# Own rows of layer 0 gathered as the unit three ahead opens, their transposes placed later in the order

## The chip, the cores and the metric

The program runs on one core of one Trainium2 chip, in one launch. The metric is the device time of that core in microseconds (us); below it is better. The kernel before was run three times without the profiler, and its time is the median of the three.

## The reference, cut to what matters

Two graph layers are computed for 8 batches of 2048 nodes with 256 channels, over one adjacency matrix with few neighbours per node (and each node its own neighbour). Each layer ends in a residual sum and a layer norm.

```python
# layer 0: scores are x W1 W2^T x^T on the edges, values are x W3
e = einsum('bnd,bmd->bnm', x @ W1, x @ W2)
e = where(adj > 0, leaky_relu(e, 0.2), -1e12)
x = layernorm(x + relu(softmax(e) @ (x @ W3)))
# layer 1: four heads of 64, scores a_src.q_i + a_dst.q_j on the edges
q = (x @ W).reshape(B, N, 4, 64)
e = where(adj > 0, leaky_relu(e_src_i + e_dst_j, 0.2), -9e15)
x = layernorm(x + elu(softmax(e) @ q))
```

## The kernel before

**Tiling.** The nodes are sorted by degree and cut into 16 tiles of 128 nodes, one node per partition. A tile `t` has `SLOTS[t]` neighbour slots, from 12 for the sparsest tile to 36 for the densest. The batches are taken in two halves `h` of four. A *unit* is one (layer, half, tile): units 0 to 15 are layer 0 of the first half, from 12 slots up to 36, units 16 to 31 layer 0 of the second half, again from 12 to 36, and then 32 units of layer 1. `K` is the unit's number of slots.

**A unit of layer 0.** `before0` gathers the tile's own 128 rows (4 KB each, tile `xo`) with an indirect DMA on POOL, copies them to the residual tile `xr` with four DMAs on SP (L531), transposes them on PE with eight 128x128 transposes (L417, tile `ps_t_x`), lets ACT copy these out (`xT`, L419), multiplies by `A` = W1 W2^T on PE (L427) and lets ACT copy the result `g` out (L542). `logits0` takes, for each slot, four dot products of the gathered neighbour rows with `g` on DVE (L562), and then a softmax. `sums0` adds up the neighbour rows with these weights on PE (L639), 16 small matmuls a slot, for which ACT makes four diagonal tiles `dg` a slot (L659). `after0` multiplies by W3, adds the residual, normalises, makes the table rows of layer 1 and writes them.

**The ring.** Neighbour rows (tile `s`) are gathered by POOL into a ring of 16 tiles of two slots (L196 is the shared gather helper). A ring tile is free again when PE has summed its slots, so POOL's gathers wait for PE (`POOL s L196 <- PE acc L639`), and DVE's dot products follow the gathers.

**The order of the work.** The program is written as generators that are stepped by `tick` (L955). A tick first lets `pump` issue ring gathers as far as there are credits, then emits up to two slots of dot products, then steps each of three lists once (twice, if the list holds more than one entry): `starts` (the `before0` of coming units), `ends` (the `after0` of finished ones) and `lists` (the neighbour lists). `sums0` emits one slot's sums and then a tick. `before0` of unit j + 3 is put into `starts` when half of unit j's slots are summed (L990), gathers at its first step, and steps four times (L534) before its transposes. POOL's order is the order in which the program emits (L346). [...] The pool of `xo` has two buffers (L170), that of `xr` three (L171). A new tile takes a buffer whose last use is over.

Of the kernel before, what the change touches and what calls it, by code (L numbers as in the profile page):

```python
# [11 lines left out]
F32 = mybir.dt.float32  # L12
# [10 lines left out]
P = 128  # L23
# [17 lines left out]
LATE = 6  # L41
# [88 lines left out]
def fast_path(  # L130
# [26 lines left out]
    NT = N // P  # L157
    KC = C // P
    HB = B // 2
    HC = HB * C  # L160
# [9 lines left out]
    xop = ctx.enter_context(tc.tile_pool(name="xown", bufs=2))  # L170
# [20 lines left out]
    def wide_tile(name):  # L191
        return wp.tile([P, 2 * QW], F32, tag="t", name=name)

    def gather(dst, table, index):

        nc.gpsimd.indirect_dma_start(  # L196
            out=dst, out_offset=None, in_=table, in_offset=AT(ap=index, axis=0),
            bounds_check=table.shape[0] - 1, oob_is_err=False,
        )
# [12 lines left out]
    xg = [tc.dram_tile([N, HC], F32, name=f"xg_{h}") for h in range(2)]  # L212
# [102 lines left out]
    order = const.tile([P, NT], I32, tag="order", name="order")  # L315
# [32 lines left out]
    def checks():  # L348

        worst = wide_tile("worst")[:, :P]  # L350
        nc.gpsimd.memset(worst, 0.0)
        bad = const.tile([P, NT + 3], F32, tag="bad", name="bad")
        found, known = bad[:, NT + 1 : NT + 2], bad[:, NT + 2 : NT + 3]
        nc.vector.tensor_scalar(bad[:, :NT], degs, 0.5, None, ALU.is_lt)
        listless = wide_tile("listless")[:, :total]
        nc.vector.tensor_scalar(listless, neg, 0.0, 0.0, ALU.is_lt, ALU.add, accum_out=found)
        nc.vector.tensor_reduce(known, degs, AX.X, ALU.add)
        nc.vector.tensor_tensor(known, known, found, ALU.add)
        nc.vector.tensor_scalar(bad[:, NT : NT + 1], known, float(total), None, ALU.not_equal)
        nc.vector.tensor_reduce(worst[:, 0:1], bad[:, : NT + 1], AX.X, ALU.max)  # L360
        yield
        pb = ps_tile("ps_bad")
        nc.tensor.transpose(pb[:, :P], worst, ident)
        yield
        most = const.tile([P, 1], F32, tag="most", name="most")
        nc.vector.tensor_reduce(most[0:1, :], pb[0:1, :P], AX.X, ALU.max)
        nc.vector.tensor_copy(flag, most[0:1, :])
        yield
        nc.vector.scalar_tensor_tensor(half, half, 2.0 * N, orderR, ALU.mult, ALU.add)
        for h in range(2):  # L370
            for j in range(2):
                nc.vector.tensor_scalar(
                    oidx[:, h, j], half, float((h * HB + j) * N), None, ALU.add
                )
# [37 lines left out]
    def transposed(src, name, dst):  # L412

        for i in range(2):
            pt = ps_tile(f"ps_t_{name}_{i}")
            for j in range(4):
                nc.tensor.transpose(pt[:, ts(j, P)], src[:, ts(4 * i + j, P)], ident)  # L417
            yield
            nc.scalar.copy(dst[:, ts(i, 512)], pt)  # L419
        yield  # L420

    def projected(srcT, weight, name, evict):
        for i in range(2):
            pp = ps_tile(f"ps_p_{name}_{i}")
            for j in range(2):
                for k in range(KC):
                    nc.tensor.matmul(  # L427
                        pp[:, ts(j, C)],
                        lhsT=srcT[:, ts((2 * i + j) * KC + k, P)],
                        rhs=weight[:, k, :],  # L430
                        start=(k == 0),
                        stop=(k == KC - 1),
                    )
            yield
            evict(i, pp)
        yield

    class Unit:
        def __init__(self, layer, h, t):
            self.layer, self.h, self.t = layer, h, t  # L440
            self.K = SLOTS[t]
            self.name = f"{layer}_{h}_{t}"

            n = self.K if self.K <= RING * CHUNK * 3 // 4 else -(-self.K // 2)
            self.parts = [(k, min(n, self.K - k)) for k in range(0, self.K, n)]
            self.chunks = [[] for _ in self.parts]
            self.p = [None] * len(self.parts)
            self.ps = [None] * len(self.parts)

            self.m, self.s = [], []  # L450
            self.ready = False


# [7 lines left out]
    clock = [0]  # L461
# [31 lines left out]
    def neighbours(t):  # L493
        K, o = SLOTS[t], offs[t]
        while t not in loaded:
            yield
        v = loaded[t].bitcast(I16)[:, :N]
        if t in up[:3]:
            numbered(loaded[t])
            nc.vector.memset(loaded[t][:, N // 2 :], 0.0)  # L500


        some = sp.tile([P, 8 * BLOCKS], F32, tag="some", name=f"some_{t}", bufs=2)
        for i in range(BLOCKS):
            nc.vector.max(some[:, ts(i, 8)], v[:, N * i // BLOCKS : N * (i + 1) // BLOCKS])
            if i % 8 == 7:
                yield
        credits[0] += 1
        rounds = -(-K // 8)
        m = sp.tile([P, 40], F32, tag="m", name=f"m_{t}")  # L510
        for i in range(rounds):
            nc.vector.max(m[:, ts(i, 8)], some)
            if i + 1 < rounds:
                nc.vector.match_replace(some, m[:, ts(i, 8)], some, 0.0)
            yield
        nc.vector.tensor_scalar(neg[:, o : o + K], m[:, :K], 0.5, LOWEST, ALU.is_lt, ALU.mult)
        far = sp.tile([P, 40], F32, tag="far", name=f"far_{t}", bufs=2)[:, :K]
        nc.vector.tensor_scalar(far, m[:, :K], 0.5, FAR, ALU.is_lt, ALU.mult)
        nc.vector.scalar_tensor_tensor(
            idx[:, o : o + K], m[:, :K], 1.0, far, ALU.subtract, ALU.add  # L520
        )
        listed[t] = True


    def before0(u):
        xo = xop.tile([P, HC], F32, tag="xo", name=f"xo_{u.name}")
        gather(xo, xg[u.h][:, :], order[:, u.t : u.t + 1])
        u.xr = xrp.tile([P, 2, HW], F32, tag="xr", name=f"xr_{u.name}")
        for r in range(2):
            for c in range(2):  # L530
                nc.sync.dma_start(  # L531
                    u.xr[64 * c : 64 * c + 64, r, :], xo[64 * r : 64 * r + 64, ts(c, HW)]
                )
        for _ in range(4):  # L534
            yield
        xT = wide_tile(f"xT_{u.name}")
        yield from transposed(xo, f"x_{u.name}", xT)
        while scored[0] < u.index - 1:
            yield
        u.g = gp.tile([P, HC], F32, tag="g", name=f"g_{u.name}")  # L540
        yield from projected(
            xT, w.A, f"g_{u.name}", lambda i, pp: nc.scalar.copy(u.g[:, ts(i, 512)], pp)  # L542
        )
        u.ready = True
# [369 lines left out]
    units = [Unit(0, h, t) for h in range(2) for t in up]  # L914
# [19 lines left out]
    for j, u in enumerate(units):  # L934
        u.index = j
    before = (before0, before1)
    logits = (logits0, logits1)
    sums = (sums0, sums1)
# [8 lines left out]
    def finish(u):  # L947
        yield from after[u.layer](u)
# [6 lines left out]
    def tick(limit):  # L955
        pump()
        while late and late[0][0] <= clock[0]:
            late.popleft()[1]()
        for _ in range(2):
            if ahead[0] < limit:  # L960
                ahead[0] += next(stream, 0)
        for queue in queues:
            for _ in range(min(len(queue), 2)):
                if queue and next(queue[0], queue) is queue:
                    queue.popleft()
        clock[0] += 1
# [5 lines left out]
    for j, u in enumerate(units):  # L972
        begun = False
        if 0 < j and j + 2 < NT:
            lists.append(neighbours(up[j + 2]))
        if j == NT:
            ends.append(checks())
        while len(ends) > 1:
            tick(0)
        if 2 <= j < 10:  # L980
            b, i = divmod(j - 2, 2)
            n = ts(i, N // 2)

            nc.gpsimd.dma_start(xg[1][n, ts(b, C)], x[HB + b, n])
        left = float(u.K)
        for share in sums[u.layer](u):
            ahead[0] -= share
            left -= share
            tick(left + units[min(j + 1, len(units) - 1)].K + LEAD)
            if not begun and left <= u.K / 2 and j + 3 < len(units):  # L990
                begun = True
                v = units[j + 3]
                starts.append(before[v.layer](v))
        ends.append(finish(u))
# [300 lines left out]
```

## Time and profile before

| what | value |
|---|---|
| time, median of three runs | 2709.94 us (2703.99 to 2711.37) |
| time of the profiled execution | 2598.36 us |
| its span, first to last instruction | 2596.3 us |
| DVE busy | 2148.3 us (83%) |
| PE busy | 1816.4 us (70%) |
| POOL busy | 1532.3 us (59%) |
| ACT busy | 1441.4 us (56%) |
| gathers of own rows, `xo` | 32, on POOL |
| gathers of neighbour rows in layer 0 | 596, on POOL |

In the span, about the first 95 us are setup, layer 0 of the first half runs to about 800 us, layer 0 of the second half to about 1595 us, and layer 1 to the end.

How to read the lines: a wait line is `engine tile line <- releaser: us in total, times, longest`. A window line gives, for a stretch of the span, the busy time of each engine and its instructions, the share of full speed that TensorE's clock was granted (PEclk), and the mean busy share of the 16 DMA engines. A timeline line gives start, duration, engine, source line, operation, output<-inputs, a count of merged instructions, and in brackets the idle time of the engine ahead of it and who ended it. `PEld` is the weight load of a matmul.

### The profile page before, as it was taken

To read this page: it belongs to the slowest core of one execution; us is meant where nothing else is said; L and a number is where in the kernel's file an instruction comes from. 1 tells how busy PE (TensorE), PEld (TensorE's weight loads), DVE (VectorE), ACT (ScalarE), POOL (GpSimd) and SP (SyncE) were. 2 spreads that over 40 slices of the span, in tenths; PEclk is the share of its full clock that TensorE was granted. 3 is DMA by queue.
4 is the path that set the end of the run, shared out by engine and by line. 5 is a ranking of instruction groups with operands and counts; after the bars stand their busy time and mean duration, and the time that the engine had idled before them with its cause. 6 is when DMAs were issued, how large, how long until landed. Compare 5 with 4: busy or idle time off the path is not lost. (4 is left out here: it accounts for less than half of the span.)

```text
span 2596.3 us, 52231 instructions
## 1 busy us (share of the span) xinstructions
PE 1816.4 (70%) x16675; PEld 989.4 (38%) x16675; DVE 2148.3 (83%) x7073; ACT 1441.4 (56%) x4849; POOL 1532.3 (59%) x1486
## 2 busy tenths in 40 slices
PE   1167797878778787788888878756475666764774
PEld 0145464545445455455555544212121222221221
DVE  6799899899889677777788885789888788988896
ACT  6245475656566556655666657454356556643455
POOL 3464455555555444535455555677677777776774
PEclk9588898989888788988898989878788788887877
DMA  9898787888875566767788768898799999987993
GB/s 382 276 338 273 257 313 267 302 285 280 269 270 194 186 218 240 247 231 235 255 264 284 257 206 273 301 342 327 273 341 355 349 339 367 349 320 270 325 358 106
DMA packets 249419, 734.92 MB, mean 283 GB/s; under 512 B 63200, under 2 KB 72544, under 8 KB 246704
## 3 DMA queue, kind: packets, MB, share of 16 engines
q0 software_dynamic: 192512, 645.89, 70.4%
q1 hardware_dynamic: 55360, 84.44, 9.6%
q8 instruction: 135, 2.21, 0.3%
q14 instruction: 148, 1.21, 0.1%
q10 hardware_dynamic: 1264, 1.18, 0.1%
HBM read 708.35 MB, written 76.09 MB: 302 GB/s over the span
## 5 line engine op out<-in xcount | busy, mean ns | idle before, releaser
L562 DVE CUSTOM_DVE_ANT_0 j<-s,g 128x256 bf16<-128x256 f32 x2384 | 1007.7, 423 | 197.7 <-DMA s<-xg,idx 127.2
L196 POOL DMA_INDIRECT s<-xg,idx x596 | 634.3, 1064 | 625.4 <-PE acc L639 413.5
L639 PE MATMUL acc<-s,ident 64*64 64x512 f32 x4768 | 610.9, 664 | 350.9 <-issue 296.7
L639 PE MATMUL acc<-s,dg 64*64 64x256 f32 x9536 | 706.1, 418 | 187.7 <-ACT dg L659 176.1
L196 POOL DMA_INDIRECT s<-qg,idx x596 | 606.7, 1018 | 242.0 <-issue 130.4
L659 ACT ACTIVATE dg<-twice,e 128x64 f32<-128x64 f32 x2384 | 617.6, 337 | 107.3 <-PE acc L639 101.8
L840 DVE TENSOR_TENSOR s<-s,p 128x2048 f32<-128x2048 f32 (+1 forms) x260 | 574.0, 2229 | 0.0
L639 PEld LDWEIGHTS acc<-s,dg 64*64 64x64 f32 x9536 | 383.1, 144 | 452.1 <-ACT dg L659 256.3
L639 PEld LDWEIGHTS acc<-s,ident 64*64 64x64 f32 x4768 | 210.4, 149 | 743.8 <-issue 600.0
L836 ACT ACTIVATE s<-s,e 128x64 f32<-128x64 f32 x1408 | 342.7, 335 | 47.7 <-DVE e L804 39.6
L395 ACT ACTIVATE z<-st,roots 128x4 f32<-128x4 f32 x64 | 19.1, 298 | 410.1 <-DVE st L384 410.1
L562 DVE DVE_READ_ACCUMULATOR2_ANT e<- 128x1 f32 x2384 | 194.0, 81 | 0.0
L204 POOL DMA_INDIRECT out_dram<-o,oidx x128 | 130.6, 1020 | 68.1 <-ACT o L407 32.2
L774 DVE TENSOR_TENSOR e<-s,own 128x32 f32<-128x32 f32 (+1 forms) x306 | 55.7, 186 | 121.5 <-DMA s<-qg,idx 120.3
L417 PE MATMUL ps_t_x<-ident,xo 128*128 128x128 f32 x256 | 55.4, 359 | 120.0 <-DMA xo<-xg,order 120.0
L723 PE MATMUL ps_q<-wqs,x1T 128*128 128x264 f32 x512 | 137.8, 407 | 2.1 <-ACT x1T L419 2.1
L427 PE MATMUL ps_p_h<-w_sb,hT 128*128 128x256 f32 x512 | 130.4, 399 | 5.6 <-ACT hT L419 5.6
L427 PE MATMUL ps_p_g<-A,xT 128*128 128x256 f32 x512 | 131.9, 404 | 1.8 <-ACT xT L419 1.5
L427 PEld LDWEIGHTS ps_p_g<-A,xT 128*128 128x128 f32 x512 | 98.0, 199 | 32.0 <-issue 8.1
L427 PEld LDWEIGHTS ps_p_h<-w_sb,hT 128*128 128x128 f32 x512 | 94.4, 194 | 40.8 <-issue 13.2
L723 PEld LDWEIGHTS ps_q<-wqs,x1T 128*128 128x128 f32 x512 | 98.3, 199 | 29.6 <-issue 7.7
L407 ACT ACTIVATE o<-xr,nmr,rstd 128x256 f32<-128x256 f32 x128 | 66.5, 589 | 76.1 <-DVE nmr L403 67.7
(138 smaller groups left out, 1467.9 us busy)
## 6 DMA issues: line engine op xcount, KB each, us to landing
adj<-in_adj_dram SPq DMA_DIRECT2D x16, 1024.0 KB
xr<-xo SPq DMA_DIRECT2D x128, 128.0 KB
x1s<-y SPq DMA_DIRECT2D x32, 512.0 KB
xr<-x1s SPq DMA_DIRECT2D x32, 512.0 KB
s<-xg,idx POOLq DMA_INDIRECT x596
s<-qg,idx POOLq DMA_INDIRECT x596
edges<-adj SPq DMA_DIRECT2D x16, 512.0 KB
xg<-in_x_dram SPq DMA_DIRECT2D x4, 2048.0 KB
```

The lines of the kernel that those rows point to most:

```text
L196: nc.gpsimd.indirect_dma_start(out=dst, out_offset=None, in_=table, in_offset=AT(ap=index, axis=0), bounds_check=table.shape[0] - 1, oob_i ...
L204: ins = nc.gpsimd.indirect_dma_start(out=table, out_offset=AT(ap=index, axis=0), in_=src, in_offset=None)
L407: nc.scalar.activation(dst[:, b, :], y[:, b, :], AF.Identity, bias=nmr[:, b : b + 1], scale=rstd[:, b : b + 1],)
L417: nc.tensor.transpose(pt[:, ts(j, P)], src[:, ts(4 * i + j, P)], ident)
L427: nc.tensor.matmul(pp[:, ts(j, C)], lhsT=srcT[:, ts((2 * i + j) * KC + k, P)], rhs=weight[:, k, :], start=(k == 0), stop=(k == KC - 1),)
L562: nc.vector.tensor_tensor_reduce(out=jt, in0=rows[:, s, ts(b, C)], in1=u.g[:, ts(b, C)], scale=1.0, scalar=0.0, op0=ALU.mult, op1=ALU.add, ...
L639: nc.tensor.matmul(out, lhsT=lhsT, rhs=rhs, start=(k == 0 and j == 0), stop=(k == K - 1 and (j == 1 or diag is None)), tile_position=(64 * ...
L659: nc.scalar.activation(diag[:, b, :], twice, AF.Copy, scale=u.p[i][:, b, k : k + 1])
L723: nc.tensor.matmul(pq[:, : C + 2 * H], lhsT=x1T[:, ts(i * KC + k, P)], rhs=w.sqs[:, k, j * H : j * H + CD + H], start=(k == 0), stop=(k == ...
L774: nc.vector.tensor_tensor(e[:, c * CHUNK : c * CHUNK + ns, :].rearrange("p s (b g) -> p s b g", b=HB), rows[:, :ns, :].rearrange("p s (b w ...
L836: nc.scalar.activation(v[:, a, g, :], v[:, a, g, :], AF.Copy, scale=pv[:, a, g : g + 1])
L840: nc.vector.tensor_tensor(v, v, pv.unsqueeze(3).to_broadcast([P, n * HB, H, D]), ALU.mult)
```

## The change

Three things are changed in layer 0.

1. The gather of `xo` is taken out of `before0` into `own_rows`, and the main loop calls it for unit j + 3 when unit j opens, before its first slot of sums, instead of when half of its slots are summed. Only units 0, 1 and 2 still gather inside `before0`. Unit 3's gather comes when unit 0 opens, that is before any step of `before0`, and so ahead of the first three neighbour lists in POOL's order.
2. In `before0`, the four steps between the copies to `xr` and the transposes become a wait of eight ticks (`LATE + 2`), two for unit 0.
3. The four DMAs to `xr` stay at the first step of `before0`.

The number of instructions, their sizes and the pools' buffers are unchanged.

```diff
+    def own_rows(u):
+        u.xo = xop.tile([P, HC], F32, tag="xo", name=f"xo_{u.name}")
+        gather(u.xo, xg[u.h][:, :], order[:, u.t : u.t + 1])
+
     def before0(u):
-        xo = xop.tile([P, HC], F32, tag="xo", name=f"xo_{u.name}")
-        gather(xo, xg[u.h][:, :], order[:, u.t : u.t + 1])
+        if u.xo is None:
+            own_rows(u)
+        xo = u.xo
         u.xr = xrp.tile([P, 2, HW], F32, tag="xr", name=f"xr_{u.name}")
...
-        for _ in range(4):
+
+        then = clock[0] + (LATE + 2 if u.index else 2)
+        while clock[0] < then:
             yield
         xT = wide_tile(f"xT_{u.name}")
         yield from transposed(xo, f"x_{u.name}", xT)
...
             nc.gpsimd.dma_start(xg[1][n, ts(b, C)], x[HB + b, n])
+        if j + 3 < 2 * NT:
+
+            own_rows(units[j + 3])
         left = float(u.K)
         for share in sums[u.layer](u):
```

More of the change, by code (lines that the diff above doesn't have):

```diff
@@ L450, in __init__ @@
             self.m, self.s = [], []
+            self.xo = None
             self.ready = False
```

## Prediction

> **What bounds the kernel now.** I read the page's busy row first: DVE is busy 83% of the span, PE 70%. Such shares are means over stages, so I next took both batch halves of layer 0 apart by windows (the second line is 870 to 1430 us, the second half):
>
> ```profile
> 200.00:710.00 510.00, 413.87 (x4128) 272.58 (x4128) 460.44 (x2259) 309.25 (x1068) 273.10 (x260) 0.89 0.83 282
> 870.00:1430.00 560.00, 451.60 (x4329) 292.86 (x4333) 418.97 (x1908) 333.15 (x1122) 262.39 (x249) 0.89 0.72 240
> ```
>
> The third busy figure is DVE: 460/510 = 90% in the first half, 419/560 = 75% in the second. PE has 81% in both. So DVE sets the pace of the first half, and something else that of the second. Then the waits, PE's and DVE's from 700 to 1450 us, and PE's from 200 to 660 and from 95 to 200:
>
> ```profile
> PE ps_t_x L417 <- DMA xo<-xg,order: 71.7, 15, 7.8
> PE acc L639 <- ACT dg L659: 59.5, 27, 5.3
> ```
>
> ```profile
> DVE j L562 <- DMA s<-xg,idx: 108.6, 79, 6.7
> ```
>
> ```profile
> PE ps_t_x L417 <- DMA xo<-xg,order: 0.5, 1, 0.5
> ```
>
> ```profile
> PE ps_t_x L417 <- DMA xo<-xg,order: 44.9, 4, 25.1
> ```
>
> PE's transposes wait for the own rows about once a unit in the second half, never in the body of the first, and at its start. Why the wait counts shows in the timelines of one such place, PE and then POOL:
>
> ```profile
> 1094.16 3.96 PE L639 MATMUL acc<-s,dg 64*64 64x256 f32 x48 [0.38 <-ACT dg L659]
> 1105.25 1.09 PE L417 MATMUL ps_t_x<-ident,xo 128*128 128x128 f32 x4 [7.13 <-DMA xo<-xg,order]
> ```
>
> ```profile
> 1096.41 1.21 POOL L196 DMA_INDIRECT xo<-xg,order  x1 [0.31 <-issue]
> ...
> 1109.36 0.99 POOL L196 DMA_INDIRECT s<-xg,idx  x1 [6.24 <-PE acc L639]
> ```
>
> POOL issues the gather 1.7 us before PE is ready for it (1105.25 - 7.13 = 1098.12). PE stands 7.13 us, frees no ring tile, POOL stands 6.24 us for a ring tile, and DVE later lacks gathered rows (the 108.6 us). Counting instructions unit by unit, I find the following (lead: from the end of the unit's dot products to the start of its sums; slack: from the end of `g` to the first dot product):
>
> | unit | wait for `xo` | slack of `g` | DVE gaps in its dots | lead |
> |---|---|---|---|---|
> | 1 / 2 | 25.1 / 4.7 | -2.1 / 1.1 | 1.1 / 0.0 | 3.6 / 16.0 |
> | 3 / 4 | 1.2 / 0 | 14.0 / 17.0 | 0.0 / 0.9 | 25.3 / 35.1 |
> | 20 | 5.9 | -2.2 | 11.4 | 42.9 |
> | 22 | 5.7 | 8.8 | 10.0 | 32.4 |
> | 24 | 7.1 | 19.4 | 11.7 | 27.2 |
> | 30 | 2.0 | 37.7 | 3.8 | 3.5 |
>
> In units 20 to 27 DVE is done 18 to 43 us before PE needs it, and still starves for rows, since the ring is full of slots that PE has not summed. PE is the pacer there, so its waits are on the path. In units 3 to 12 DVE's gaps are 0 to 4 us: there it is the path itself.
>
> **The gather, moved forward.** Units 15 to 31 but 18 wait 74.6 us in all (16 waits of 2 to 8 us). In the change the gather leaves POOL half a unit earlier, and PE asks for it eight ticks after mid-unit instead of four steps after: at least 6 + 8 slots of sums between them, each 16 matmuls in 1.09 us of PE alone, and 2 to 3 us with the rest of the unit's work (a pitch of 46 us for unit 24's 18 slots and some 4 further ticks, 2.1; its transposes and products, a tick apart, start at 1105.25, 1108.98, 1111.89 and 1114.61, 3.1). That is some 30 us against the 8.8 us that the row shows from issue to use (1096.41 to 1105.25). The wait goes to zero. [...]
>
> **The clock after a stall.** Windows around the same place (the figure before the DMA share is PEclk):
>
> ```profile
> 1098.00:1105.20 7.20, 0.12 (x2) 0.00 (x0) 4.78 (x24) 2.56 (x11) 4.21 (x4) 0.78 1.03 409
> 1105.20:1109.20 4.00, 3.95 (x26) 2.59 (x27) 2.51 (x11) 1.67 (x5) 0.00 (x0) 0.54 0.73 288
> 1109.20:1117.00 7.80, 7.80 (x63) 6.23 (x62) 7.15 (x35) 6.31 (x19) 4.25 (x4) 1.00 0.69 225
> ```
>
> After the stall PE works at half speed for 3 to 6 us; summed over these units 73 us, that is 36 us of lost work. [...] PE's side of the gain is then 75 + 36 = 111 us at most.
>
> **What is late next.** DVE. At the first half's 90% its 419 us need 464, so 96 us is the most that the window of 560 allows. PE would then hold (452 - 30)/464 = 91%. No row shows both engines over 90% together; the nearest has 81% and 90%. Per unit (21 to 27) the pitch is 44.6 us, PE's without wait and half speed 44.6 - 5.6 - 2.0 = 37.0, DVE's without its gaps 34.3; but units 28 to 31 need 51.3 of DVE against a pitch of 51.2, and unit 30's lead is only 3.5. So the path changes sides near the end, and PE still waits for `dg`. I take 60 us, about 60% of the smaller bound; ends 0 and 96.
>
> **Transposes later.** Four more ticks, an estimated 8 to 13 us (two to three us a tick, as above), put `g` that much later. Units 19 to 23 lose their slack (-3 to 13 us) and DVE will show waits for `g`. Their leads (32 to 44 us) cover that; without them it would cost up to 10 us a unit. In units 3 to 14, where DVE is the path, slack is 14 to 41 us: nothing.
>
> **Buffers and queues.** With two `xo` buffers, unit j + 3's gather waits for unit j + 1's transposes and its `xr` copies, and behind it on POOL stand the ring's gathers and the table scatters. The copies of units 3 to 29 were issued 20 to 60 us before that opening, the transposes earlier still: nothing; it would cost what the copies slip beyond 20 us. SP's copies keep their place and find the rows there (from 900 to 1430 us SP waited once for them, 10.5 us). POOL has the same instructions, one 1.3 us gather half a unit sooner, covered by its 208 us of waiting for PE in that window.
>
> **The start.** Unit 3's gather now stands ahead of the first lists: 1.3 us of POOL, or its 0.5 MB at the 370 GB/s that the queue moved there, 1.4 us, in full on the path, as DVE idles for the first list until 101.1 us. It also holds one of the two buffers while units 0 to 2 share the other, and unit 1 and 2's transposes come six ticks later. DVE is busy 95 of 105 us there. At best (PE idle, transposes run on landing) only the 1.4 us are lost. At worst unit 1's `g` comes behind three slots of unit 0's sums (150.7 + 3.3 + 8.3 = 162 against 148: 14) and unit 3's behind unit 1's (another 6): 21 in all. I take 8, nearer the low end, because PE was idle half of that window.
>
> **The sum.** -60 + 8 = -52 us, from a span of 2596.3 (profiled time 2598.36, so 2 us lie around it) to about 2544. The median of the runs is 112 us above the profiled time, and no row says where; I carry the 52 over unscaled: 2709.94 - 52 = 2658.
>
> **The rivals.**
> - *Most of it is taken back by DVE and `dg`*: unit 30's lead of 3.5 us and PE's 59.5 us of waits for `dg` speak for it. Then only 5 to 30 us net come through: 2680 to 2705. Chance 0.20.
> - *DVE closes all its gaps*: -96 + 1 to 10, 2615 to 2625. The first half shows that 90% can be held. Chance 0.08.
> - *Slower*: the crowded start. Place: the two `xo` buffers with unit 3's rows in one, before unit 0's dots. Price: 21 us, up to 12 more if unit 2's gather (behind four more ring gathers, 5.6 us) also delays the list work. It decides once the later stage gives back less than that: if the pitch there stays with the ring's round trip, about 2720. Against it: DVE has list work to fill such gaps. Chance 0.17.
> - *The rows still come late*, because POOL reaches the opening no earlier relative to PE: excluded nearly, the distance is counted in slots of PE's own order; it is inside the second case's low end.
>
> **Numbers.** The likeliest (0.55) is 2635 to 2678 with 2658. The range 2615 to 2718 reaches over the rivals. A measurement can tell 0.3%, 8 us. Faster by more: 0.55 + 0.08 + half of 0.20 = 0.73; within: the other half and 0.02 of the slower case, 0.12; slower: 0.15.
>
> **What would show it.** PE's wait for `xo` in the second half gone, PEclk there above 0.89, POOL's wait for PE and DVE's for gathered rows well below 208 and 109 us, waits of DVE for `g` in units 18 to 23 without a later start of their sums, DVE at 85% or more from 870 us on. Wrong if DVE's share stays at 75%, if POOL waits for the copies at the openings, or if the first half ends over 20 us later.

## The result, and the profile after

| | median | spread | ratio to before, 95% interval |
|---|---|---|---|
| before | 2707.15 us | 2693.03 to 2711.37 | |
| after | 2689.04 us | 2681.93 to 2703.03 | 0.9948 [0.9926, 0.9969] |

The kernel is faster, by 14 us (2707.15 x 0.0052) where 52 were forecast. The profiled execution of after took 2691.09 us, and its span is 2689.3.

One thing has to be set right before the two traces can be compared. The profiled execution of before from which the prediction was made took 2598.36 us, about 110 less than the same kernel takes otherwise. A second profile of the kernel before (span 2727.8 us, the first experiment) is therefore what after is compared with here.

Windows of the first half (200 to 710 us) and the second (870 to 1430 us), first in the second profile of before:

```profile
200.00:710.00 510.00, 428.61 (x4034) 278.15 (x4035) 451.67 (x2214) 301.85 (x1034) 263.19 (x255) 0.89 0.83 275
870.00:1430.00 560.00, 464.74 (x4369) 300.18 (x4361) 417.43 (x1902) 332.43 (x1111) 262.02 (x252) 0.90 0.72 237
```

and after:

```profile
200.00:710.00 510.00, 424.10 (x3789) 261.82 (x3785) 440.78 (x2159) 288.25 (x979) 246.32 (x236) 0.91 0.76 258
870.00:1430.00 560.00, 491.31 (x4753) 306.42 (x4753) 461.77 (x2088) 355.49 (x1230) 290.65 (x275) 0.95 0.77 260
```

Read the counts in brackets as progress. In the second half PE gets through 4753 matmuls instead of 4369 in the same 560 us, its clock is 0.95 instead of 0.90, and DVE is busy 461.77 instead of 417.43 us. That is the gain that was meant. In the first half the counts go the other way: 3789 matmuls for 4034, 2159 DVE instructions for 2214. Something there became slower.

The waits of PE and DVE from 700 to 1450 us, in the second profile of before:

```profile
PE ps_t_x L417 <- DMA xo<-xg,order: 46.5, 13, 5.5
PE acc L639 <- ACT dg L659: 27.5, 14, 4.3
```

```profile
DVE j L562 <- DMA s<-xg,idx: 102.1, 67, 6.8
```

and after (PE, then DVE):

```profile
PE acc L647 <- ACT dg L667: 47.2, 21, 4.9
PE acc L647 <- issue: 18.1, 41, 1.2
```

```profile
DVE j L570 <- DMA s<-xg,idx: 26.2, 21, 2.5
...
DVE j L570 <- ACT g L550: 4.9, 5, 1.7
```

PE's wait for the own rows is gone, and DVE's wait for gathered rows falls by 76 us. PE waits 20 us more for `dg`, the next thing that is late. DVE's waits for `g` are small (4.9 us, 3.4 in the second profile of before).

POOL's waits from 870 to 1430 us, before (second profile) and after:

```profile
POOL s L196 <- PE acc L639: 225.4, 82, 13.1
```

```profile
POOL s L196 <- PE acc L647: 191.5, 86, 12.1
```

The two halves can be told apart by two marks that I take from the traces (all in us): the start of unit 16's dot products, and the end of layer 0's sums.

| | unit 2's dots | unit 16's dots | end of layer 0 | between the last two |
|---|---|---|---|---|
| before, second profile | 186.1 | 838.8 | 1622.2 | 783.4 |
| after | 195.4 | 865.6 | 1601.9 | 736.3 |

So the second half is 47 us shorter and the first 27 longer. The sum is 20 us at the end of layer 0, near the 14 that the timed runs show. (Layer 1, which the change doesn't touch, took 1105.6 and 1087.4 us in these two executions. Over all kernels below it took 1087 to 1106, and no kernel's layer 1 is read as a difference.)

### The profile page after: what moved, and what is told of

Same layout as the page of the kernel before. It is cut to its first block, busy times and chain, and to the rows that moved or that the text cites. A ratio compares the mean times of both kernels' runs of the same rounds, so it can differ in the third digit from the quotient of the medians.

```text
span 2689.3 us, 52275 instructions
## 1 busy us (share of the span) xinstructions
PE 2078.2 (77%) x16675; PEld 1093.7 (41%) x16675; DVE 2163.6 (80%) x7073; ACT 1445.6 (54%) x4849; POOL 1526.7 (57%) x1486
## 4 chain that ended last, share of the span: by engine, by line
PE 25%; DVE 22%; issue 22%; DMA 8%; POOL 6%; ACT 4%; another core or an unknown queue 1%; POOLq 0%; DVEq 0%; ACTq 0%
PE acc L647 22%; DVE j L570 14%; POOL s L196 4%; DMA s<-qg,idx 4%; DMA s<-xg,idx 3%; DVE s L848 2%; DVE e L570 1%; ACT s L844 1%; DVE st L384 1%; PE ps_q L731 1%; PE ps_p_h L427 1%; ACT dg L667 1%; DVE y L707 1%; DMA nb<-edges,order 1%
## 5 line engine op out<-in xcount | busy, mean ns | idle before, releaser
L647 PE MATMUL acc<-s,ident 64*64 64x512 f32 x4768 | 821.3, 675 | 227.3 <-issue 199.4
L647 PE MATMUL acc<-s,dg 64*64 64x256 f32 x9536 | 757.4, 408 | 176.7 <-ACT dg L667 111.5
L667 ACT ACTIVATE dg<-twice,e 128x64 f32<-128x64 f32 x2384 | 624.0, 337 | 158.1 <-PE acc L647 103.2
L647 PEld LDWEIGHTS acc<-s,ident 64*64 64x64 f32 x4768 | 314.9, 149 | 725.3 <-issue 668.6
L647 PEld LDWEIGHTS acc<-s,dg 64*64 64x64 f32 x9536 | 392.6, 139 | 481.1 <-issue 181.2
L731 PE MATMUL ps_q<-wqs,x1T 128*128 128x264 f32 x512 | 151.9, 433 | 28.4 <-ACT x1T L419 13.8
L798 ACT ACTIVATE e<-e 128x288 f32<-128x288 f32 (+11 forms) x34 | 14.8, 435 | 175.8 <-DVE e L797 84.1
```

Source lines behind the costliest of these rows:

```text
L647: nc.tensor.matmul(out, lhsT=lhsT, rhs=rhs, start=(k == 0 and j == 0), stop=(k == K - 1 and (j == 1 or diag is None)), tile_position=(64 * ...
L667: nc.scalar.activation(diag[:, b, :], twice, AF.Copy, scale=u.p[i][:, b, k : k + 1])
L731: nc.tensor.matmul(pq[:, : C + 2 * H], lhsT=x1T[:, ts(i * KC + k, P)], rhs=w.sqs[:, k, j * H : j * H + CD + H], start=(k == 0), stop=(k == ...
```

## The experiments

**Theory and rival.** *Theory:* both steps of the sum, -60 in the second half and +8 at the start, hold more or less, and what is missing was lost in units 3 to 14, where the prediction booked nothing for the later transposes. *Rival:* the start is dearer than 8 us, or the second half gives less than 60. A second rival is that the atypical profile of before misled the whole sum.

The kernel before was run again beside each group of experiments, and its median lay between 2700.67 and 2723.4 us from one occasion to the next. So kernels are compared by their ratios to it, not by their times, and a difference of some 0.8% (7 us at unit 16) between marks from two occasions says nothing.

**1. The kernel before, once more** (no edit).

> The kernel before, unchanged, profiled a second time. The profile of before that the prediction read had a span of 2596.3 us, 113 us under the median of its timed runs, and layer 1 took 1001 us there against 1087 us in the profile of the changed kernel. Theory A (that one execution was untypical and layer 1 is the same for both kernels): span about 2700 us, layer 1 about 1085 us, layer 0 over near 1610 to 1620 us, with DVE paced as before. Theory B (the changed order costs layer 1 some 85 us): layer 1 again about 1000 us. Ratio to the kernel before 1.000 in both.

Measured: 2720.32 us beside 2723.4, ratio 0.9991 [0.9977, 1.0005]; the profiled execution 2730.05 us. So the first profile was one odd execution of the same kernel. What made it fast isn't known. For the sizes the second rival stays: the wait for the own rows from 700 to 1450 us was 71.7 us in the odd profile and is 46.5 here.

**2 to 4. The parts alone.** The early gather with the four steps kept:

```diff
-        then = clock[0] + (LATE + 2 if u.index else 2)
-        while clock[0] < then:
+        for _ in range(4):
             yield
```

> Half of the change: own rows gathered as the unit three ahead opens, transposes again four steps after the start of before0. Theory A (the start and the first half of layer 0 lose 20 to 50 us because the transposes come later and g is late for DVE): the loss is gone and the second half's gain stays, 40 to 50 us under before (ratio 0.982 to 0.985), unit 2's dot products begin near 175 us. Theory B (the loss is that unit 3's rows hold one of the two buffers and stand ahead of the first lists): no better than the full change, 14 to 18 us under before, unit 2's dot products begin near 195 us.

the late transposes alone:

```diff
-        if j + 3 < 2 * NT:
-            own_rows(units[j + 3])
```

> The other half of the change: the gather stays in before0 at mid-unit, only the transposes wait eight ticks. Theory A (four ticks, 8 to 13 us, are enough for a gather that needs 9 us, and the loss at the start comes from them): PE's wait for own rows in the second half nearly gone (under 15 us), the start as late as in the full change, and the time equal to it, 14 to 18 us under before. Theory B (the early gather is what removes the wait): the wait stays at 40 us or more in the second half and the time is at or above before.

and the whole change in units 16 to 31 only:

```diff
-        then = clock[0] + (LATE + 2 if u.index else 2)
+        if u.index < 16:
+            for _ in range(4):
+                yield
+        then = clock[0] + (LATE + 2 if u.index >= 16 else 0)
...
-        if j + 3 < 2 * NT:
+        if 16 <= j + 3 < 2 * NT:
```

> The whole change, but for units 16 to 31 alone (the second batch half); units 0 to 15 as before. Theory A (the change gains about 45 us in the second half and loses 20 to 50 us in the first): 40 to 50 us under before (ratio 0.982 to 0.985). Theory B (the first half loses nothing by itself, the second gains only what the timed runs show): 14 to 18 us under before, as the full change.

Measured: the gather alone 2683.84 us, 0.9849 [0.983, 0.9868]. Late transposes alone 2712.03, 0.9957 [0.9941, 0.9973]. Units 16 to 31 alone 2671.2, 0.9813 [0.9793, 0.9833], which is -51 us. The second half's step was nearly right. Half of the change is worth more than the whole, and what spoils it is in the first half and comes with the late transposes: unit 16's dots start at 843.1 us with the gather alone and at 867.5 with the late transposes alone.

Either part alone takes the wait away: with the late transposes alone PE doesn't wait for the own rows from 700 to 1450 us either, and the second half takes 749.8 us where before took 783.4. So in the whole change the ticks were not needed beside the early gather.

**5 to 8. Where in the first half.** Early gathers everywhere; the eight ticks only for units 1 to 3, only for units 4 to 15, or twelve for those; and gathers early only from unit 4 on, with four steps. The diff is that of units 1 to 3; the next two have `4 <= u.index <= 15` in it, and the second of them 12 for 8; the last has `4 <= j + 3 < 2 * NT` at the gather.

```diff
+        late_one = 1 <= u.index <= 3
+        if not late_one:
+            for _ in range(4):
+                yield
+        then = clock[0] + (8 if late_one else 0)
```

> All gathers early, transposes eight ticks late for units 1 to 3 alone, four steps for all others. With gather_only at 0.985 (about 41 us under before) and the full change at 0.995. Theory A1 (the loss is made at the start, where g of units 1 to 3 comes late for a busy DVE, and is only carried on): nearly all of the difference is here, 15 to 20 us under before (0.993 to 0.995), and unit 16's dot products begin 20 us or more after gather_only's 843 us. Theory A2 (most of it is made unit by unit in units 4 to 15): a cost of 7 to 10 us, 31 to 34 us under before (0.988).

> All gathers early, transposes eight ticks late for units 4 to 15 alone, the body of the first half, where g has 14 to 40 us of slack before its first dot product. Theory A1: no cost, as gather_only (0.985). Theory A2 (although no dot product waits long for g, the dots are emitted and ordered later, DVE is the pacer, and ACT and PE wait for DVE's softmax): a cost of 15 to 20 us, 21 to 26 us under before (0.990 to 0.992), unit 16's dot products at 858 to 865 us.

> The same as late4to15 with twelve ticks instead of eight, so a delay of eight ticks over the four steps where late4to15 has four. Theory A1: still no cost while g has slack, at most 5 us under late4to15's gain. Theory A2: the cost grows with the delay, roughly doubles, 30 to 40 us over gather_only, that is 0 to 10 us under before.

> Early gathers from unit 4 on, four steps for all, so that the start is as before: unit 3's rows no longer stand ahead of the first neighbour lists and no longer hold one of the two buffers. gather_only began its first dot product 2.2 us later than before (120.5 against 118.3). Theory: 2 to 4 us better than gather_only, 43 to 46 us under before (0.983 to 0.984). Rival (the place of unit 3's gather costs nothing once DVE has caught up): equal to gather_only, 0.985.

| | us | ratio, 95% interval | unit 16's dots |
|---|---|---|---|
| eight in 1 to 3 | 2681.03 | 0.987 [0.9851, 0.989] | 839.5 |
| eight in 4 to 15 | 2702.02 | 0.9927 [0.9907, 0.9947] | 868.6 |
| twelve in 4 to 15 | 2699.68 | 0.9928 [0.9911, 0.9945] | 865.2 |
| early gather from 4, four steps | 2676.94 | 0.9844 [0.9824, 0.9864] | 840.8 |

The late transposes of the start cost 0.987 - 0.9849, some 6 us, and the intervals overlap. Those of units 4 to 15 cost 0.9927 - 0.9849, some 21 us. With the gather alone the two add up to the whole change, 0.9849 + 0.0021 + 0.0078 = 0.9948, which leaves nothing for the ticks of units 16 to 31. That the sum meets 0.9948 exactly is luck, as each ratio is known to 0.002. That twelve ticks cost no more than eight was not expected: the price is not so much a tick.

**9 to 11. Three attempts at the cause.** Does the late work collide with the finishing work of the unit before it, which begins at the same place? Then moving that too should help. In `after0`, for units 1 to 12:

```diff
         while evictions:
             evictions.popleft()()
+        for _ in range(4 if 1 <= u.index <= 12 else 0):
+            yield
```

> The kernel with early gathers and four steps, and in addition the finishing work (evicted sums transposed, W3, residual, norm, table rows) of units 1 to 12 begins four ticks later. It is the control for the next kernel: here the preparation's transposes already come before the unit's end, so moving the finishing work away gains nothing. Theory collision (the late transposes and g projections of unit j + 3 fall beside the finishing work of unit j): 2675 to 2690, as without it. Theory lateness itself: the same. If the finishing work's place matters by itself: over 2695.

> Early gathers, eight ticks for units 4 to 15, and the finishing work of units 1 to 12 also begins four ticks later, so that both stand to each other as with four steps. Theory collision: the 21 us that eight ticks cost come back, 2675 to 2690, equal to the control, and unit 16's dot products start at about 843 us. Theory lateness itself (g or x's transposes being late costs, whatever stands beside them): 2698 to 2712, start of unit 16's dot products at about 867 us.

and no ticks at all in units 4 to 15, with 0 in place of 8 in the diff above:

> Early gathers, and units 4 to 15 take no ticks at all between the copies and the transposes (unit 16 on keeps four steps). It is the other end of the series of 0, 4, 8 and 12 ticks. Theory collision: equal to four steps or up to 8 us faster, since all of the preparation then lies clear of the unit's end: 2670 to 2685. Theory lateness itself, with a price per tick up to eight: some 15 to 20 us faster than four steps, 2660 to 2668.

Measured: the control 2698.99 us, 0.9925 [0.9898, 0.9951]; with eight ticks 2701.93, 0.9932 [0.9906, 0.9958]; without ticks 2665.82, 0.981 [0.9781, 0.9839]. The test of the collision says nothing, since its control is itself dear: delaying the finishing work by four ticks costs about 20 us where the late transposes are not there to collide with. It does show that this piece of work isn't free to move in this stage either.

**12. Both halves as they are best so far**: early gathers from unit 4, four steps up to unit 15, eight ticks from 16.

> The candidate for the best: early gathers from unit 4 on, four steps for units up to 15 and eight ticks from unit 16. If the gain lies in the second half alone and early gathers are free in the first, this equals the kernel with the change in units 16 to 31 alone: 2665 to 2680. If the eight ticks are of no use in the second half either, it equals early gathers with four steps everywhere, which is the same range; if early gathers help the first half a little, 2655 to 2665.

Measured: 2678.24 us, 0.9867 [0.9833, 0.9901], a wide interval. Its profiled execution had unit 16's dots at 833.7 and 732.7 us from there, as good as the best; the timed runs spread from 2663 to 2686. It is not shown to be better than units 16 to 31 alone.

**13 and 14. The lists.** One wait differed between all the good and all the bad kernels so far (24 to 44 us against 58 to 78). POOL's waits from 250 to 870 us, with the early gather and four steps:

```profile
POOL s L196 <- PE acc L646: 122.6, 63, 7.3
...
POOL s L196 <- DVE some L506: 43.7, 9, 12.4
```

and with eight ticks in units 4 to 15:

```profile
POOL s L196 <- PE acc L651: 121.2, 55, 7.2
POOL s L196 <- DVE some L506: 68.0, 10, 14.8
```

In the first half units load a neighbour list into a ring tile, and POOL, when it comes to that tile again, stands until DVE has gone over the list (`some`). It stands 24 us longer with eight ticks, about what is lost. The next two kernels take this wait away, one with four steps and one with eight ticks: the lists, but for the first three, get a buffer of their own (`list_tile`, of a ring tile's size), and the ring has 15 tiles instead of 16.

```diff
-    ring = ctx.enter_context(tc.tile_pool(name="ring", bufs=RING))
+    ring = ctx.enter_context(tc.tile_pool(name="ring", bufs=RING - 1))
+    nbp = ctx.enter_context(tc.tile_pool(name="nbown", bufs=1))
...
-    credits = [RING]
+    credits = [RING - 1]
...
-        r = ring_tile(f"nb_{t}")
+        if t in up[:3]:
+            r = ring_tile(f"nb_{t}")
+        else:
+            r = list_tile(f"nb_{t}")
+            credits[0] += 1
...
-        credits[0] += 1
+        if t in up[:3]:
+            credits[0] += 1
```

> Early gathers, four steps, and the neighbour lists (but the first three) lie in a buffer of their own instead of a ring tile; the ring has 15 tiles instead of 16. It is the base of the pair. POOL's waits for DVE's list passes should be gone after unit 3. The shorter ring costs something in the second half, so the whole time says little (2670 to 2720); unit 16's dot products should start at 830 to 850 us.

> The same with eight ticks for units 4 to 15. Theory lists (what eight ticks cost is POOL standing at the ring tile that holds a list, in order, until DVE has gone over it): equal to own_list_four within 8 us, unit 16's dot products within 8 us of its start. Rival (the late transposes cost PE, ACT and DVE time by their place, POOL's waits only follow): 15 to 25 us slower than own_list_four, unit 16's dot products 20 to 25 us later.

Measured: 2624.26 us, 0.9713 [0.9685, 0.9741] with four steps, and 2643.46, 0.9787 [0.9753, 0.9821] with eight ticks; unit 16's dots at 795.9 and 815.8. POOL's waits from 250 to 870 us, with eight ticks:

```profile
POOL s L200 <- PE acc L660: 188.6, 93, 7.1
POOL s L200 <- issue: 33.8, 111, 0.3
POOL s L200 <- PE ps_t_x L421: 13.8, 17, 1.2
POOL s L200 <- remote: 10.5, 11, 1.5
```

The wait for `some` is gone, and eight ticks still cost 20 us. So POOL's stops at the lists were not the cause. A difference in waits that matched the loss closely was no proof. But taking the lists out of the ring is worth a good deal by itself, or so it seemed.

**15. No ticks in either half**, early gathers from unit 4.

> Early gathers from unit 4 on, and from unit 4 on the transposes follow the copies without any tick between, in both halves. If the gain comes from the early gather alone, this is as fast as the best so far, 2658 to 2672, with unit 16's dot products at 833 to 838 us and 732 to 738 us from there to the end of layer 0. If the second half needs distance between gather and transposes, PE waits for the own rows again there (over 20 us) and the time is 2680 to 2700.

Measured: 2650.02 us, 0.9795 [0.9773, 0.9817]; 837.2 us at unit 16, 722.5 from there to the end of layer 0, against 734.3 with eight ticks in that half. The early gather alone is enough in both halves: from 200 us on PE doesn't wait for the rows, although no tick separates copies and transposes.

**16 to 18. What the lists' buffer is worth to whom**: with the kernel before, with the whole change, and with early gathers without ticks.

> The kernel before, with the neighbour lists (but the first three) in a buffer of their own and 15 ring tiles. If the buffer acts on the first half alone, about 47 us of it are gained there (unit 16's dot products at about 795 us against 839 to 843) and PE still waits for the own rows in the second half: 2650 to 2675. If the early gather is needed for it, 2690 or more.

> The whole change with the lists' own buffer. The late transposes cost about 20 us in units 4 to 15 here too and the second half gains: 2628 to 2650, unit 16's dot products at 812 to 822 us. If they cost nothing without the lists in the ring: 2610 to 2625.

> The best candidate: early gathers from unit 4 on, no ticks between copies and transposes, lists in their own buffer. Both gains together: 2605 to 2622, unit 16's dot products at 788 to 797 us. If they overlap: as own_list_four, 2620 to 2630.

Measured, with the ratio to the kernel before; in the third line units 0 to 3 are left as they were (their rows at mid-unit, four steps), and the fourth is experiment 13:

| with the lists' own buffer | us | ratio, 95% interval | unit 16's dots | from there to layer 0's end |
|---|---|---|---|---|
| kernel before | 2731.94 | 1.0107 [1.0069, 1.0144] | 846.1 | 787.7 |
| whole change | 2664.3 | 0.9855 [0.9824, 0.9886] | 823.0 | 742.0 |
| early gather, no ticks | 2634.49 | 0.9751 [0.972, 0.9781] | 807.3 | 721.3 |
| early gather, four steps | 2624.26 | 0.9713 [0.9685, 0.9741] | 795.9 | 721.9 |

The first line is the most telling of all. The buffer was expected to gain by itself (2650 to 2675 us), and the time fell into the other case, 2690 or more. The buffer alone makes the kernel 1.1% slower, the early gather alone makes it 1.5% faster, both together 2.9%. PE's waits of the kernel before with the lists' own buffer, from 200 to 660 us:

```profile
PE acc L648 <- ACT dg L668: 37.8, 16, 5.2
PE ps_t_x L421 <- DMA xo<-xg,order: 25.6, 7, 5.2
```

In the same window the second profile of before has 4.3 us of the wait for `xo`, and with buffer and early gather together there is none, while the wait for `dg` is the same as here (35.5 us). So POOL's stops at the lists had kept everything else late enough for the rows to be in time. With the stops gone (24.3 us of `some` from 250 to 830 us in the second profile of before, none here), the rows are what is late. That wait is 25.6 of the 50 us by which unit 16's dots come later than with both (846.1 and 795.9). The rest isn't accounted for, and nothing here separates the buffer from the ring that is one tile shorter, nor was the buffer tried with late transposes alone, which also take the wait for the rows away.

The last line is the lowest ratio of all that ran. Its interval overlaps with that of the line above it, so the two can't be told apart.

The whole change against early gathers without ticks, both with the lists' own buffer, differs by about 1.0% (0.9855 to 0.9751, intervals apart), 16 us of it before unit 16 (823.0 to 807.3) and 21 behind it (742.0 to 721.3). Most of the first part and all of the second lie in the late transposes, so they cost in the second half as well. (The first part also has the start in it, some 6 us above.)

## Why the prediction was wrong, point by point

*The gather moved forward: right.* PE's wait for `xo` is zero from 700 us on. The rows come in time even without ticks between (experiment 15), so the estimate of 30 us against 8.8 was on the safe side. The second profile of before has 46.5 us of that wait from 700 to 1450 us, and all of it went.

*The clock after a stall: right in direction.* PEclk goes from 0.90 to 0.95 in the second half, over 560 us an estimated 28 us of full-speed work at most, where 36 were booked. (The 73 us at half speed from which the 36 come are what the clock's records in the prediction's profile show at 0.5 behind the start of the transposes of units 15 to 31, 3.0 to 6.1 us a unit. They are reached only with 3.9 us after unit 18's transposes, which had not waited. Without them it is 69, and 35 of lost work.)

*60 us for the second half: a little high.* 47 in the traces, 51 with the change in units 16 to 31 alone. The two bounds, 0 and 96, held. DVE rose to 461.77/560 = 82%, not 85%. The sum was made from the odd profile, whose wait for the rows was half as long again (71.7 us for 46.5), so that 60 came near is in part luck.

*Buffers and queues: nothing.* No wait of POOL's gather of `xo` for the copies shows at the openings (POOL idles 3.8 us in all before its 13 gathers of `xo` from 870 to 1430 us, at most 0.3 us before one), and POOL's wait for PE fell from 225.4 to 191.5 us. (The prediction's 208 is of 900 to 1430 us, where after has 181.5: below it, but not "well below".)

*The start, 8 us: right in size.* Unit 2's dots start 9.3 us later. By timing the late transposes of units 1 to 3 cost some 6 us, within the uncertainty of none.

*"Transposes later. ... In units 3 to 14, where DVE is the path, slack is 14 to 41 us: nothing." This is the step that failed.* These late transposes cost 21 us, where the prediction had put nothing, of the 38 us by which the forecast missed (52 - 14). 9 to 13 more are the 60 that was 47 to 51. The text's own condition fired: "Wrong if ... the first half ends over 20 us later", and it ended 27 later.

The reasoning had asked only who waits for `g`. Nobody does: with eight ticks in units 4 to 15 the slack of `g` in units 9 to 14 is still 19 to 32 us, and the waits of DVE from 200 to 850 us name no `g`. But PE's own time was booked as free, because DVE had the higher busy share. The prediction's own profile says otherwise, when units follow each other:

| unit, prediction's profile | dots end | its sums start | sums of the unit before end |
|---|---|---|---|
| 10 | 536.88 | 553.46 | 550.28 |
| 12 | 628.00 | 641.99 | 642.17 |
| 13 | 681.26 | 692.78 | 692.96 |
| 14 | 732.25 | 744.74 | 744.92 |

From unit 12 on the sums start as those of the unit before end, with the dots 12 to 14 us done: PE is what the sums wait for. The second profile has the same (unit 12's sums start at 669.37 us, those of unit 11 end at 669.55). Before that, from unit 4 to unit 9, it has gaps of 6.5 to 7.6 us between two units' sums, and PE is busy in all of them. This is the one before the sums of unit 6, whose dots ended at 375.43:

```profile
395.91 1.96 PE L639 MATMUL acc<-s,dg 64*64 64x256 f32 x32
397.80 1.99 PE L427 MATMUL ps_p_g<-A,xT 128*128 128x256 f32 x8
399.63 1.05 PE L723 MATMUL ps_q<-wqs,x1T 128*128 128x264 f32 x4
400.52 1.89 PE L427 MATMUL ps_p_g<-A,xT 128*128 128x256 f32 x8
402.25 2.83 PE L723 MATMUL ps_q<-wqs,x1T 128*128 128x264 f32 x12
405.01 1.09 PE L639 MATMUL acc<-s,dg 64*64 64x256 f32 x16
```

The leads of 25.3 and 35.1 us for units 3 and 4 stood in the prediction's table and said so already. A DVE at 90% was coupled through the ring (POOL waits 135.2 us for PE's sums from 250 to 830 us in the second profile) to a PE that had work at every place where the products could go.

What the delay does to PE can be counted. I cut the sums of units 4 to 14 at half of each unit's slots and added up the time of all first and all second halves, with PE's products of `xT` and `A` that fall into them:

| kernel | first halves | second halves | products in first / second |
|---|---|---|---|
| early gather, four steps | 199.0 us | 297.1 us | 0 / 160 |
| the same, eight ticks | 247.9 us | 274.9 us | 160 / 16 |
| own list buffer, four steps | 192.3 us | 272.5 us | 0 / 160 |
| own list buffer, eight ticks | 243.5 us | 240.1 us | 160 / 16 |

Eight ticks carry the products out of the unit's second half into the first slots of the next unit, where the finishing work begins as well. There they cost 49 and 51 us; where they left, only 22 and 32 come back. Without the lists' buffer the largest items of PE are: the products themselves 41 us in and 37 out, the sums in the first halves 12 us longer (113.9 to 125.9), in the second halves 4 us shorter, table-row work in the second halves 6 us longer, PE's idle time there 11 us longer (39.2 to 49.7). Twelve ticks fall into the same first halves, which is why they cost no more (240.9 and 283.6 us), and with four the work stays in the second (0 and 160 products).

So a place and a size are shown, in two pairs of kernels. It isn't one wait: PE's waits in the stretch from the start of unit 9's sums to that of unit 15's come to some 42 and 43 us, while its busy time grows, as these windows show, with four steps

```profile
540.53:819.06 278.53, 236.23 (x2414) 145.96 (x2416) 247.36 (x1180) 171.96 (x612) 152.95 (x143) 0.92 0.81 271
```

and with eight ticks

```profile
548.01:843.27 295.26, 251.09 (x2429) 154.53 (x2432) 248.03 (x1175) 174.33 (x614) 149.94 (x143) 0.92 0.76 255
```

PE is busy 15 us longer at the same mean clock, 0.92; DVE's work is the same 247 to 248 us. Sixteen more products of `A` fall into the second stretch and take 5 of the 15 us. The other 10 are in the sums, busy 150.9 and 160.6 us for the same 2000 matmuls, and each of these takes as long as before (415 and 417 ns in the mean). So they overlap less (some 830 us of matmuls lie in 150.9 and in 160.6 us), and why is open. A collision with the finishing work fits the place, but its test had a control that was itself dear, and I don't count it as shown. It is also open why the second half gains 15 us (736.5 to 721.9, of which the two occasions may make 6) from a change to lists that it doesn't have.

In units 16 to 31, where the prediction took the leads to cover four more ticks, four and eight ticks took the same (736.5 and 736.3 us). No ticks at all took 12 us less than eight (722.5 and 734.3, again from two occasions), so nothing was to be had from the ticks there either.

*The rivals.* The gain that "DVE and `dg`" would take back was to end at 2680 to 2705, and the time did (2689.04), but by luck and not for that reason: PE's wait for `dg` rose by 20 us in a half that gained 47 all the same. The slower case's mechanism, the crowded start, was there and small.

## What to carry to other kernels

When a step is moved later, ask not only who waits for its result but what the engine that runs it does at its new place: a slack of 20 us in the result says nothing on the engine's own time. Whether two parts of a change are both needed shows only when each runs alone: here either took the wait away, and one of them cost. Which engine paces a stage is read from who starts when the other ends (the sums began as the unit before ended), not from the higher busy share. And a wait that is absent from a stage may only be hidden behind another: POOL's stops at the lists hid the late rows of the first half, and the two repairs changed the time by -1.5% (early gather) and +1.1% (own buffer) alone and by -2.9% together.

## What the runs showed of the hardware that was not expected

One execution of a program can stand far from all others: the profiled one of the kernel before took 2598.36 us, while its timed runs, on all occasions, lay between 2693 and 2731. Most of it is in layer 1 (1001 us instead of 1087 to 1106) and some in the first half of layer 0 (unit 16's dots at 815.3 instead of 838.8 us in the second profile); the second half of layer 0 took 779.5 instead of 783.4. The granted clock was not the reason, as it was lower, 0.850 for 0.865. What the lines show is that PE's matmuls of layer 1's sums overlapped more:

```profile
L639 PE MATMUL acc<-s,ident 64*64 64x512 f32 x4768 | 610.9, 664 | 350.9 <-issue 296.7
L639 PE MATMUL acc<-s,ident 64*64 64x512 f32 x4768 | 848.6, 674 | 215.7 <-issue 169.8
```

The first is the odd profile, the second the other one: 4768 matmuls of nearly the same length (664 and 674 ns in the mean) kept PE busy for 610.9 and 848.6 us. Why they did is open. When a profile's own time stands that far from the timed runs, sums made from it are not to be trusted.
